# A mixture's routing with the last two batches one turn further apart, and second-choice rows added tile by tile

## The chip, the cores and the metric

The kernel runs on one core of a Trainium2 chip. The metric is device microseconds of one execution, as the median of several. A profile is a separate execution under the hardware profiler, with its own time. The engines are named as in the profile: PE (TensorE), DVE (VectorE), ACT (ScalarE), POOL (GpSimd) and SP (SyncE, which only issues transfers here).

## The reference

Activations of 4 batches by 512 tokens by 128 features go through four layers. Each is a half-weighted mixture of experts or gated block, an attention or scan, and the same mixture again. All is float32. What the change touches is the mixture of the last layer, which stands once before and once after that layer's attention:

```python
def _moe_forward(x, wg, w1, b1, w2, b2):          # T = 2048 tokens, E = 8, K = 2, H = 512
    cap = int(K * CAP_FACTOR * ((T + E - 1) // E))    # 512 slots for each expert
    scores = jax.nn.softmax(xt @ wg, axis=-1)
    gates_k, idx_k = jax.lax.top_k(scores, K)
    gates_k = gates_k / jnp.sum(gates_k, axis=-1, keepdims=True)
    m = jnp.transpose(jax.nn.one_hot(idx_k, E), (1, 0, 2)).reshape(K * T, E)
    loc = jnp.sum((jnp.cumsum(m, axis=0) - 1) * m, axis=-1).reshape(K, T).T
    valid = loc < cap                                 # first choices of all tokens, then second choices
    disp = zeros((E, cap, D)).at[idx_k, clip(loc)].add(xt * valid)
    h = jax.nn.relu(einsum('ecd,edh->ech', disp, w1) + b1)
    out = einsum('ech,ehd->ecd', h, w2) + b2
    return einsum('tk,tkd->td', gates_k * valid, out[idx_k, loc])
```

A token's place at its expert is its rank among all tokens that chose that expert, so the batches are ranked one after the other; second choices take the places behind the first ones.

## The kernel before

**Tiles.** A batch is four tiles of 128 tokens. The class `Mixture` makes one mixture in three steps: `tokens` (routing and scatter), `experts`, `combine`. There are four: f00 and f01 with one choice (layer 0), f30 and f31 with two (layer 3). f30 is the "third mixture", before the last attention; f31 is the last stage of the kernel.

**Routing.** `tokens` is a generator; each `yield` ends a turn. For one batch it does, in order: layer norm (statistics on DVE, L160 and L161; rs, rstd and off on POOL, L164 to L169; the norm itself on ACT, L174), four transposes on PE (L187) and a copy nT (L313), eight small matmuls for the logits (L322), the two choices on DVE (L218 to L231, with the exponential on ACT, L340), a running count (scan L354 and cum L388), the rank as six matmuls on PE (L365, L367, L371), and on DVE kept, at, slot and to (L392 to L401), the row of the scatter table for every token. Then POOL copies the gates beside the rows (L405) and issues the scatters to DRAM (L408), four for each choice and batch. The rank of a batch needs `cum`, the counts of the batches before it.

**Order.** In the stage before f30, `behind` runs the second layer's blocks for two pairs of batches. The first pair's tokens go through one generator with each scatter in a turn of its own. The second pair's batches 2 and 3 have one generator each, run by `skewed`: one turn of each live generator in every round, batch 3 starting some rounds after batch 2. In this stage POOL keeps the order in which the program issues its instructions; for PE, DVE, ACT and SP a planner sets the order when the kernel is built, in view of the order of issue. At run time every engine goes through its instructions in order, so one that waits holds all behind it. Copies of attention weights (wmixed, L901, and wqkvT, L134) are placed among the end of this stage.

**Experts.** When f30 or f31 is scattered, SP fetches for each expert two tables of 512 rows (L439), one for each choice, as four tiles of 128 rows by W = 130 columns. First choices are laid from the front of an expert's places and second ones from the end, so `behind[:, e, s]`, a flag of 0 or 1 for each row, says whether the second table's row counts. In a first-choice row the 128 features come first and two columns (place and gate) last; in a second-choice row the two columns come first. `prepare(e)` merges both on DVE:

```python
nc.vector.tensor_tensor(d2, d2, bc(behind[:, e, :], [P, per, W]), ALU.mult)      # L449
nc.vector.tensor_tensor(d[:, :, :D], d[:, :, :D], d2[:, :, 2:], ALU.add)         # L450
nc.vector.tensor_tensor(d[:, :, D:], d[:, :, D:], d2[:, :, :2], ALU.add)         # L451
```

Then PE transposes the four tiles (dT, L455), ACT copies dT to SBUF (L457), and DVE makes the rows for the way back (lost, L461; back, L464). The expert itself is the up product h_f (L479), a relu on ACT (L483) and DVE (L484), the down product o_f (L515), the bias on DVE (L495), the gate on ACT (L500) and the scatter of results on POOL (L501). `prepare(e + 1)` is issued after the h_f of expert e. Each of the two tables has three buffers; the next fetch into one waits for its last reader.

Of the kernel before, what the change touches and what calls it, by code (L numbers as in the profile page):

```python
# [12 lines left out]
ALU = mybir.AluOpType  # L13
# [4 lines left out]
P = 128  # L18
D = 128
# [11 lines left out]
W = D + 2  # L31
# [10 lines left out]
def kernel(ctx: ExitStack, tc: tile.TileContext, a: dict, out: bass.AP):  # L42
    nc = tc.nc
# [12 lines left out]
    def bank(name):  # L56
        return psum.tile([P, 512], FP, name=name, tag="bank", bufs=8)
# [147 lines left out]
    def bc(ap, shape):  # L205
        while len(ap.shape) < len(shape):
            ap = ap.unsqueeze(len(ap.shape))
        return ap.to_broadcast(shape)
# [28 lines left out]
    class Mixture:  # L237
# [180 lines left out]
        def experts(self, w, beside=None):  # L418

            w1, b1T, w2, b2 = w  # L420
            cap, per, whole, left = self.cap, self.per, self.cap // P, self.cap % P
            with tc.tile_pool(name=f"moe_{self.tag}", bufs=2) as pool:
                if self.k == 2:
# [5 lines left out]
                    behind = pool.tile([P, E, per], FP, name=f"behind_{self.tag}", tag="behind", bufs=1)  # L429
# [14 lines left out]
                def prepare(e):  # L444
                    tag = f"{e}_{self.tag}"
                    d = got[e, 0]
                    if self.k == 2:
                        d2 = got[e, 1]
                        nc.vector.tensor_tensor(d2, d2, bc(behind[:, e, :], [P, per, W]), ALU.mult)  # L449
                        nc.vector.tensor_tensor(d[:, :, :D], d[:, :, :D], d2[:, :, 2:], ALU.add)  # L450
                        nc.vector.tensor_tensor(d[:, :, D:], d[:, :, D:], d2[:, :, :2], ALU.add)  # L451
                    ps = bank(f"dT{tag}")
                    for s in range(per):
                        m = min(P, cap - s * P)
                        nc.tensor.transpose(ps[:, s * P : s * P + m], d[:m, s, :D], ident[:m, :m])  # L455
                    dT = pool.tile([P, cap], FP, name=f"dT{tag}", tag="dT")
                    nc.scalar.copy(dT, ps[:, :cap])  # L457

                    back = pool.tile([P, per], I32, name=f"back{tag}", tag="back", bufs=8)
                    lost = pool.tile([P, per], FP, name=f"lost{tag}", tag="lost", bufs=4)  # L460
                    nc.vector.scalar_tensor_tensor(  # L461
                        lost, d[:, :, D], 0.0, astray[:, e * per : (e + 1) * per], ALU.is_equal, ALU.mult
                    )
                    nc.vector.tensor_tensor(back, d[:, :, D], lost, ALU.add)  # L464
                    made[e] = d, dT, back
# [4 lines left out]
                for e in range(E):  # L470
# [3 lines left out]
                    d, dT, back = made[e]  # L474
# [12 lines left out]
                    if e + 1 < E:  # L487
                        prepare(e + 1)
# [83 lines left out]
    def padded(pool, i):  # L572
        v = pool.tile([P, NT, NH, SLOT], FP, name=f"vpad{i}", tag=f"vpad{i}", bufs=1)
        nc.gpsimd.memset(v, 0.0)
        nc.gpsimd.memset(v[:, :, :, HD : HD + 1].rearrange("p t h o -> p (t h o)"), 1.0)
        return v
# [435 lines left out]
    def prep_l1():  # L1012
        l1["gate"] = load_T(a["L1_ffn_gate_weight"], E, D, "gate1T")
        l1["wg"] = load_T(a["L1_ffn_w_gate"].rearrange("e i h -> (e i) h"), E * I1, D, "wg1T")
        l1["wu"] = load_T(a["L1_ffn_w_up"].rearrange("e i h -> (e i) h"), E * I1, D, "wu1T")
        l1["sg"] = load_T(a["L1_ffn_ws_gate"], D, D, "sg1T")
        l1["su"] = load_T(a["L1_ffn_ws_up"], D, D, "su1T")
        sd = load_T(a["L1_ffn_ws_down"], D, D, "sd1T")
        raw = stage.tile([P, E, I1], FP, name="raw_wd1", tag="raw")
        nc.sync.dma_start(raw, a["L1_ffn_w_down"].rearrange("e h i -> h e i"))  # L1020
        ps = bank("wd1")
        for c in range(NC):
            nc.tensor.transpose(
                ps[:, c * P : (c + 1) * P], raw[:, 2 * c : 2 * c + 2, :].rearrange("p e i -> p (e i)"), ident
            )
        wd = pools["w"].tile([P, NC, D], FP, name="wd1T", tag="wd1T")
        copy(wd, ps.rearrange("p (c d) -> p c d", d=D))
        l1["down"] = [wd[:, c, :] for c in range(NC)] + [sd]

        raw = stage.tile([P, D], FP, name="raw_qk1", tag="raw")  # L1030
        for i, s in enumerate(("q", "k")):
            nc.sync.dma_start(raw[i * NH * R1 : (i + 1) * NH * R1, :], a[f"L1_attn_W{s}1"])
        ps = bank("qk1")
        nc.tensor.transpose(ps[:, :D], raw, ident)
        qk1 = pools["w"].tile([P, D], FP, name="qk1T", tag="qk1T")
        copy(qk1, ps[:, :D])
        l1["factors"] = [qk1] + [load_T(a[f"L1_attn_W{s}2"], NH * R2, D, f"w{s}2T") for s in ("q", "k")]
        l1["wv"] = load_T(a["L1_attn_Wv"], D, D, "wv1T")
        l1["wo"] = load_T(a["L1_attn_Wo"], D, D, "wo1T")
        l1["bo"] = load_row(a["L1_attn_bo"], "bo1")  # L1040
# [339 lines left out]
    l3 = {}  # L1380
# [83 lines left out]
    def whole(parts):  # L1464
        for _ in parts:
            pass

    def skewed(gens, lag):

        live = {i: g for i, g in enumerate(gens)}  # L1470
        r = 0
        while live:
            for i in list(live):
                if r >= i * lag and next(live[i], "end") == "end":
                    del live[i]
            r += 1
            yield
# [24 lines left out]
    with tc.tile_pool(name="tables", bufs=1) as tables:  # L1502
# [19 lines left out]
        f30 = Mixture("f30", CAP3, 2)  # L1522
        l0_attn(f00.combine, emptied(f01, f30), lambda b: f01.tokens([b], gate0T, fine=True))
    with tc.tile_pool(name="weights12", bufs=1) as mid:
        pools["w"] = mid
        prep_l1()
        with tc.tile_pool(name="raw2", bufs=1) as pool:
            made = prep_l2(pool)
            next(made)
            next(made)  # L1530
            f01.experts(l0["w"], made.send)
            whole(made)
        first = small.tile([P, 1], FP, name="first_sigmoid", tag="first_sigmoid", bufs=1)
        nc.scalar.activation(first, l2["m"][:, 0, 0:1], AF.Sigmoid)
        for b in range(NB):
            whole(f01.combine(b))
        with tc.tile_pool(name="ahead1", bufs=2) as ahead:
            vpads[:] = [padded(ahead, 0), None]
            begun = l1_begin(ahead)

            def followed(pool, bs):
                yield from l1_ffn(pool, 0, bs)
                if bs[0] == 0:

                    yield from begun[0](0)
                    for g in range(2):
                        begun[1](0, g)
                        yield
                        begun[4][0, g] = begun[2](0, g)

            with tc.tile_pool(name="ffn10", bufs=2) as pool:
                whole(skewed([followed(pool, bs) for bs in pairs], 12))

            l1_attn(lambda pool: prep_l3_ffn(xs[0]), begun)

        def behind(pool, bs):
            yield from l1_ffn(pool, 1, bs)
            yield from l2_ffn(pool, 0, bs)
            yield from l2_attn(pool, bs)
            yield from l2_ffn(pool, 1, bs)  # L1560
            if bs[0] == 0:

                parts = f30.tokens(bs, l3["gate"], "scalar", pool, apart=True)
                while next(parts, "end") != "end" and next(parts, "end") != "end":
                    yield
            else:
                yield from skewed([f30.tokens([b], l3["gate"], "scalar", pool) for b in bs], 3)

        with tc.tile_pool(name="chain", bufs=2) as pool:
            decay = pool.tile([P, S], FP, name="decay", tag="decay", bufs=1)  # L1570
            nc.gpsimd.memset(decay, 0.9)
            for bs in pairs:
                l2["gates", bs[0]] = pool.tile([P, 2 * NT, P], FP, name=f"gates{bs[0]}", tag=f"gates{bs[0]}", bufs=1)
                nc.gpsimd.memset(l2["gates", bs[0]], 0.0)

            l2["row"] = []
            for u in range(E // 4):
                flag = pool.tile([P, 1], FP, name=f"flag{u}", tag=f"flag{u}", bufs=1)
                nc.vector.tensor_reduce(flag, ident.rearrange("p (r c) -> p r c", c=SLOT)[:, :, u], AX.X, ALU.add)
                row = pool.tile([P, P], FP, name=f"row{u}", tag=f"row{u}", bufs=1)  # L1580
                nc.vector.tensor_copy(row, flag.to_broadcast([P, P]))
                l2["row"].append(row)
            with tc.manual_schedule(engines={mybir.EngineType.Pool}):
                whole(skewed([behind(pool, bs) for bs in pairs], 8))
        pools["w"] = wpool
# [54 lines left out]
```

## Time and profile before

| | us |
|---|---|
| median of three runs (1532.04 to 1535.4) | 1533.77 |
| the profiled execution | 1513.06 |
| its span, first to last instruction | 1511.3 |
| granted TensorE clock in it, mean share of full speed | 0.911 |

| stretch of the span | us | PE busy | DVE busy | POOL busy | granted clock |
|---|---|---|---|---|---|
| batches 2 and 3 are routed, up to batch 2's first scatter (974.9 to 991.5) | 16.6 | 7.69 | 6.65 | 8.28 | 0.75, then 0.50 |
| their scatters (991.5 to 1013.4) | 21.9 | 3.51 | 3.97 | 16.46 | 0.50 |
| fetch and first preparation of f30 (1013.4 to 1021.25) | 7.85 | 1.09 | 3.42 | 4.69 | 0.50 |
| experts of f30 (1021.25 to 1075.3) | 54.05 | 54.05 | 25.91 | 25.36 | 0.97 |
| fetch and first preparation of f31 (1423.65 to 1430.06) | 6.41 | 1.09 | 3.33 | 0.00 | 0.50 |
| experts of f31 (1430.06 to 1484.5) | 54.44 | 54.44 | 24.87 | 25.24 | 0.96 |

Times in the span are microseconds from its start, durations of single instructions nanoseconds where so marked. A line of a timeline gives start, duration, engine, source line and operation, what is written and read, how often, and in brackets the idle time of that engine before it and what ended it. In the chain of waits each line is a start, a duration and the work that the next line waited for. Where a wait has several causes, the named one is the last by this profile and may not be the one that counted. L numbers are lines of the kernel before; in the changed kernel the edited operation stands at L450 to L454, and lines behind it are three higher.

### The profile page before, as it was taken

Reading aid. Unit: us, or ns where it says so; the run is one execution under the profiler, and the core shown is the slowest. Engines: PE = TensorE matmul, PEld = TensorE weight load, DVE = VectorE, ACT = ScalarE, POOL = GpSimd, SP = SyncE. Lnnn points to the kernel's source line nnn. Section 1 sums busy time; section 2 is a strip of 40 time slices with the busy share of each in tenths; the row PEclk is TensorE's granted clock in tenths of the full one; section 3 lists DMA queues with packets and bytes.
Section 4 is the critical chain, followed back from the end, with each engine's and each line's share of the span. In section 5 each row is a group of like instructions: output and inputs, shape, how many; then the busy total and the mean of one; then the engine's idle time right before and its main releaser. Section 6 shows DMA issues by size and latency. Waiting matters only on the chain.

```text
span 1511.3 us, 28774 instructions
## 1 busy us (share of the span) xinstructions
PE 1271.2 (84%) x10645; PEld 816.7 (54%) x10645; DVE 880.3 (58%) x2890; ACT 682.8 (45%) x1431; POOL 694.0 (46%) x808
## 2 busy tenths in 40 slices
PE   4787999995969999999878878729689999998394
PEld 3465666774746666667555656616433333333173
DVE  5236767763355657767456566525367787774343
ACT  1235877871422367767522222103236655564042
POOL 5346767871433678868323111464431223312343
PEclk9897999995999999999999888759879999999597
DMA  9410240002513884231022000023105000000223
GB/s 262 101 53 22 79 170 12 9 7 73 151 37 65 223 258 145 87 121 44 4 64 49 1 1 1 28 71 91 60 15 177 15 7 10 14 3 15 78 78 112
DMA packets 100660, 106.21 MB, mean 70 GB/s; under 512 B 9084, under 2 KB 73832, under 8 KB 100520
## 3 DMA queue, kind: packets, MB, share of 16 engines
q1 hardware_dynamic: 91752, 90.11, 20.7%
q0 software_dynamic: 6656, 13.22, 2.5%
q8 instruction: 84, 1.38, 0.4%
q10 hardware_dynamic: 2112, 1.05, 0.3%
q14 instruction: 56, 0.46, 0.1%
HBM read 62.49 MB, written 41.85 MB: 69 GB/s over the span
## 4 chain that ended last, share of the span: by engine, by line
PE 70%; DVE 9%; POOL 8%; DMA 5%; issue 5%; ACT 3%; SPq 1%; POOLq 0%; ACTq 0%; DVEq 0%
PE s_a L610 13%; PE t_a L655 10%; PE o_f L515 6%; PE h_f L479 6%; PE acc_a L677 5%; PE acc_a L749 5%; PE y_f L1329 3%; PE t_a L610 3%; POOL disp_f L408 2%; PE ot_a L768 2%; PE gu_f L1092 2%; PE lg_f L322 1%; POOL rstd_f L165 1%; DVE low L699 1%; PE gu_f L1093 1%
## 5 line engine op out<-in xcount | busy, mean ns | idle before, releaser
L642 POOL TENSOR_SCALAR sc_a<-sc_a,top_a 128x128 f32<-128x128 f32 (+3 forms) x256 | 274.8, 1089 | 84.7 <-DVE top_a L627 55.8
L610 PE MATMUL s_a<-k_a,q_a 32*128 32x512 f32 (+3 forms) x1536 | 263.4, 544 | 7.0 <-DVE top_a L631 3.7
L719 ACT ACTIVATE w_a<-t_a 128x512 f32<-128x512 f32 x256 | 140.4, 595 | 116.6 <-PE t_a L610 86.9
L699 DVE TENSOR_REDUCE low<-s_a 128x1 f32<-128x512 f32 x256 | 163.4, 684 | 45.4 <-PE t_a L610 32.7
L655 PE MATMUL t_a<-ident,sc_a 128*128 128x128 f32 x1280 | 174.3, 283 | 4.3 <-DVE top_a L631 3.8
L610 PE MATMUL t_a<-ql_a,k_a 32*128 32x512 f32 x512 | 167.2, 644 | 0.3 <-DVE low L699 0.2
L501 POOL DMA_INDIRECT res_f<-y_f,back_f x112 | 109.8, 980 | 124.6 <-ACT y_f L500 90.3
L655 PEld LDWEIGHTS t_a<-ident,sc_a 128*128 128x128 f32 x1280 | 144.6, 144 | 41.0 <-issue 16.5
L644 ACT ACTIVATE sc_a<-sc_a,top_a 128x128 f32<-128x128 f32 (+3 forms) x256 | 135.0, 575 | 12.8 <-DVE top_a L631 12.2
L610 PEld LDWEIGHTS s_a<-k_a,q_a 32*128 32x128 f32 x1536 | 91.5, 187 | 79.1 <-issue 41.9
L664 ACT ACTIVATE w_a<-t_a 128x256 f32<-128x256 f32 (+2 forms) x192 | 94.2, 526 | 71.0 <-PE t_a L655 70.8
L408 POOL DMA_INDIRECT disp_f<-n_f,to_f x96 | 94.8, 988 | 56.2 <-issue 35.8
L515 PE MATMUL o_f<-w_l,h_f 128*128 128x128 f32 (+1 forms) x896 | 109.6, 277 | 0.0
L515 PEld LDWEIGHTS o_f<-w_l,h_f 128*128 128x128 f32 (+1 forms) x896 | 102.1, 184 | 8.0 <-DVE back_f L464 4.4
L479 PE MATMUL h_f<-dT_f,w_l 128*128 128x320 f32 (+1 forms) x256 | 104.1, 544 | 2.8 <-ACT dT_f L457 2.8
L677 PE MATMUL acc_a<-w_a,vpad 128*32 128x128 f32 x2560 | 98.2, 280 | 0.0
L666 ACT COPY w_a<-t_a 128x256 f32<-128x256 f32 (+2 forms) x192 | 93.5, 527 | 5.0 <-PE t_a L655 4.7
L631 DVE CUSTOM_DVE_ANT_0 sc_a<-s_a,future 128x128 f32<-128x128 f32 (+3 forms) x128 | 62.3, 487 | 47.7 <-PE s_a L610 39.0
L1147 POOL TENSOR_TENSOR h_f<-h_f,cb_f 128x512 f32<-128x512 f32 x32 | 40.7, 1286 | 104.4 <-DVE h_f L1098 62.7
L631 DVE CUSTOM_DVE_ANT_0 sc_a<-s_a,table 128x128 f32<-128x128 f32 (+3 forms) x128 | 62.3, 487 | 43.5 <-PE s_a L610 38.3
L500 ACT ACTIVATE y_f<-o_f,d_f 128x128 f32<-128x128 f32 (+1 forms) x112 | 39.0, 394 | 98.0 <-DVE o_f L495 94.1
L749 PE MATMUL acc_a<-w_a,vpad 128*32 128x256 f32 x1024 | 82.1, 391 | 1.0 <-DVE low L699 0.9
(341 smaller groups left out, 2182.8 us busy)
## 6 DMA issues: line engine op xcount, KB each, us to landing
fac_a<-fac_a_sb SPq DMA_DIRECT2D x36, 256.0 KB, 4.9
disp_f<-zeros_f SPq DMA_DIRECT2D x4, 2080.0 KB, 10.6
d_f<-disp_f SPq DMA_DIRECT2D x32, 260.0 KB, 3.0
w_l<-in_L_ffn_w_dram SPq DMA_DIRECT2D x16, 512.0 KB, 7.2
cb_f<-rows_f SPq DMA_DIRECT2D x16, 512.0 KB, 8.4
q_a<-fac_a SPq DMA_DIRECT2D x32, 256.0 KB, 3.5
k_a<-fac_a SPq DMA_DIRECT2D x32, 256.0 KB, 3.8
r_f<-res_f SPq DMA_DIRECT2D x16, 256.0 KB, 2.8
```

The costliest lines, as they stand in the source:

```text
L408: nc.gpsimd.indirect_dma_start(out=self.to[c][i0 + t][:, :], out_offset=bass.IndirectOffsetOnAxis(ap=to[:, c, t : t + 1], axis=0), in_=ns[ ...
L479: nc.tensor.matmul(ps[u][:, :cap], w1[:, e, (c + u) * P : (c + u + 1) * P], dT, start=True, stop=True)
L515: nc.tensor.matmul(po[:m, s, :], h[:, c, s * P : s * P + m], w2[:, e, c, :], start=(c == 0), stop=(c == NC - 1),)
L610: nc.tensor.matmul(ps[:, n0:n1], q[r : r + SLOT, i * P : (i + 1) * P], k[r : r + SLOT, n0:n1], start=True, stop=True)
L631: nc.vector.tensor_tensor_reduce(sc, banks[r][:, :n], more, -1.0, HUGE, ALU.add, ALU.min, top)
L642: nc.gpsimd.tensor_scalar(sc, sc, top, None, ALU.subtract)
L644: nc.scalar.activation(sc, sc, AF.Exp, bias=top, scale=-1.0)
L655: nc.tensor.transpose(ps[:, x * n + j * P : x * n + (j + 1) * P], st["sc", u, i, r0 + x][:, j * P : (j + 1) * P], ident,)
L677: nc.tensor.matmul(st["acc", u][r * SLOT : (r + 1) * SLOT, i * P : (i + 1) * P], vpads[b % 2][:, j, g * 4 + r, :], st["w", u, i, r][:, j * ...
L699: nc.vector.tensor_reduce(st["low", u][:, i, c : c + 1], ps, AX.X, ALU.max, negate=True)
L719: nc.scalar.activation(w, ps, AF.Exp)
L749: nc.tensor.matmul(acc[r * SLOT : (r + 1) * SLOT, n0:n1], vpads[b % 2][:, j, g * 4 + r, :], st["w", u, j, r][:, n0:n1], start=(j == 0 and ...
```

## The change

Two edits. In `behind`, batch 3's routing begins four rounds after batch 2's instead of three. In `prepare`, the whole second-choice table is no longer multiplied by its flag and then added; for each of the four tiles one operation multiplies the 128 features of a second-choice row by the row's flag and adds them to the first-choice row. Only the two columns beside them are still multiplied and added for all four tiles at once. The edit in `prepare` holds for both f30 and f31.

```diff
@@ prepare(e), in experts
                     if self.k == 2:
                         d2 = got[e, 1]
-                        nc.vector.tensor_tensor(d2, d2, bc(behind[:, e, :], [P, per, W]), ALU.mult)
-                        nc.vector.tensor_tensor(d[:, :, :D], d[:, :, :D], d2[:, :, 2:], ALU.add)
+                        for s in range(per):
+                            nc.vector.scalar_tensor_tensor(
+                                d[:, s, :D], d2[:, s, 2:], behind[:, e, s : s + 1], d[:, s, :D], ALU.mult, ALU.add
+                            )
+                        nc.vector.tensor_tensor(d2[:, :, :2], d2[:, :, :2], bc(behind[:, e, :], [P, per, 2]), ALU.mult)
                         nc.vector.tensor_tensor(d[:, :, D:], d[:, :, D:], d2[:, :, :2], ALU.add)
                     ps = bank(f"dT{tag}")
@@ behind(pool, bs)
             else:
-                yield from skewed([f30.tokens([b], l3["gate"], "scalar", pool) for b in bs], 3)
+                yield from skewed([f30.tokens([b], l3["gate"], "scalar", pool) for b in bs], 4)
```

`skewed`, which the number goes to:

```python
def skewed(gens, lag):
    live = {i: g for i, g in enumerate(gens)}
    r = 0
    while live:
        for i in list(live):
            if r >= i * lag and next(live[i], "end") == "end":
                del live[i]
        r += 1
        yield
```

## Prediction

> **What bounds the kernel now.** I read the page first (PE 84% busy, 70% of the chain of waits), then the chain around the two third-layer mixtures, then each engine's timeline there. The scatter stage ahead of the third mixture (f30) is not PE's. In the chain of waits from 930 to 1100 us (start, duration, what):
>
> ```profile
> 982.85 0.23 POOL rs_f L164
> ...
> 984.83 0.50 ACT n_f L174
> 985.37 1.63 PE T_f L187 x4
> 987.00 0.32 PE rank_f L365 x2
> ...
> 990.54 0.10 DVE to_f L401
> ...
> 996.72 1.07 POOL disp_f L408
> ...
> 1011.14 2.27 DMA disp_f<-n_f,to_f
> ...
> 1015.39 4.41 DMA d_f<-disp_f
> ...
> 1021.25 5.35 PE h_f L479 x8
> ```
>
> Batch 3's norm and transposes stand ahead of batch 2's rank, then come the scatters, the fetch and the experts. The timelines of DVE and POOL say why:
>
> ```profile
> 981.96 0.19 DVE L388 TENSOR_TENSOR cum_f<-cum_f,pre_f 128x16 f32<-128x16 f32 x1
> 988.21 0.22 DVE L392 SCALAR_TENSOR_TENSOR kept_f<-rank_f,masks_f 128x64 f32<-128x64 f32 x1 [6.07 <-PE rank_f L371]
> 990.48 0.17 DVE L401 TENSOR_TENSOR to_f<-slot_f,spare_f 128x8 int32<-128x8 f32 x1
> 991.50 1.12 POOL L408 DMA_INDIRECT disp_f<-n_f,to_f  x1 [6.46 <-DVE masks_f L226]
> 1002.28 0.98 POOL L408 DMA_INDIRECT disp_f<-n_f,to_f  x1 [0.17 <-POOL wmixed_l L901]
> ```
>
> Batch 2's choices were finished at 982.15, but DVE then sat 6.07 us until its rank had left PE, where it was queued behind batch 3's transposes (985.37). POOL sat 6.46 us with nothing to scatter, and then issued batch 2's and batch 3's 16 scatters back to back, 1.26 us apart, to 1012.10. The end of this stage is set by when that train starts.
>
> The other edit is read at the fourth mixture (f31), DVE and PE timelines:
>
> ```profile
> 1426.69 0.70 DVE L449 TENSOR_TENSOR d_f<-d_f,behind_f 128x520 f32<-128x520 f32 x1 [16.10 <-DMA d_f<-disp_f]
> 1427.43 0.69 DVE L450 TENSOR_TENSOR d_f<-d_f,d_f 128x512 f32<-128x512 f32 x1
> 1428.22 1.09 PE L455 MATMUL dT_f<-ident,d_f 128*128 128x128 f32 x4 [18.63 <-DMA d_f<-disp_f]
> 1430.06 5.74 PE L479 MATMUL h_f<-dT_f,w_l 128*128 128x512 f32 x8 [0.75 <-ACT dT_f L457]
> ```
>
> PE does nothing until both whole-tile operations are through. By the order of instructions its wait is on L450 (end 1428.12); the DMA named is another that landed then. From 1430.06 PE is busy without a gap to 1484.5 (the stretch shows 54.44 of 54.44 us), as it is from 1021.25 to 1075.30 in f30: whatever starts the first expert earlier ends the stage earlier.
>
> [...] an idle TensorE falls back to half clock. The windows show it: granted clock 0.50 from 985.4 to 1021.25, so matmuls here are priced cold. [...] L408 lasts 0.96 us and lands 2.27 us after its start.
>
> **Part 1: four turns instead of three.** Nothing is added or removed. The order of instructions shows on PE batch 2's six rank matmuls ahead of batch 3's four transposes; on DVE batch 2's targets wholly ahead of batch 3's maxima, and two statistics of batch 3 moved between batch 2's choices; on POOL one of the two wmixed copies (L901, 0.30) ahead of batch 3's scatters instead of behind them. ACT and SP keep their order.
>
> Worked forward from the trace. The moved statistics put about 0.35 us into batch 2's choices: masks at 981.95, scan at 982.3. Batch 3's own statistics end at 980.0 instead of 979.16; POOL reads them at 982.85, behind six scatters, so that costs nothing. The rank starts at 982.0 and takes, cold, 0.69+0.43+0.43 (batch 3's at 992.75) = 1.55: 983.55. Targets: in f31 kept to L401 took 1.31 with 0.2 of other work between, so 1.1: 984.7. From targets to the first scatter took 0.81 (958.16 minus 957.35) and 0.85 (batch 2): **985.5, not 991.50**. POOL is free at 985.05.
>
> Batch 2's eight scatters then end at 985.5+10.08 = 995.6. Ahead of batch 3's stand two L405 (0.32), both wmixed (0.58) and a gap of 0.17: 996.67. Are batch 3's targets there? Its transposes stay at 985.37 (set by POOL's L169 and ACT), since the rank has left PE 1.8 us before; nT at 987.62, logits cold 1.88 as in f31 (1403.09): 989.5; maxima to masks 2.66 as in f31: 992.2; rank 1.55; kept to targets 1.9 with the wqkvT copy between: 995.7, plus 0.81 = 996.5. Just inside POOL's 996.67. So the last train starts at 996.7 instead of 1002.28: **-5.6 us**. After it stand only the last landing, the fetch and the experts, all released by it, and no other transfer runs there. Bounds: -4.6 if batch 3's targets are 1.2 us later than I work out; -6.0 if both trains keep their distance.
>
> **Part 2: rows times flag, tile by tile.** Per expert: out go L449 (128x520, 0.70) and L450 (128x512, 0.69); in come four scalar_tensor_tensor of 128x128 and one small multiply of 128x8 (0.16). L451 stays. 16 experts in both mixtures: 80 in for 32 out. No row has the new form. Pieces: a pointer operand adds 0.06 (L1368 749 against L1338 690 ns); at 128 columns, L178 with two of them lasts 0.34:
>
> ```profile
> 350.68 1.12 DVE L178 TENSOR_SCALAR n_f<-x,mv_f,rstd_f 128x128 f32<-128x128 f32 x4 [1.47 <-POOL rstd_f L165]
> ```
>
> I take these: first done at 0.34, fourth at 1.12, against 1.43 for the dependent pair. On top, each transpose now has its own wait for its own operation. In f31: first transpose at 0.40, four cold ones 1.09: through at 1.49 us after the data, against 2.62 before (1429.31 minus 1426.69). **-1.1**. In f30 the transposes came 0.32 after L450's end, where PE's first wait after the pools are exchanged is a long list: 0.66+1.09 = 1.75 against 2.83 (1020.45 minus 1017.62): **-1.1**. For the other seven experts nothing is won: PE is busy and their preparation lies under matmuls, 26 us of DVE work in 54. Bounds for each mixture: -0.35 if the transposes only run after the fourth operation (2.27 against 2.62); -1.3 with cheaper operations. [...] Behind the new DVE instructions stand the next expert's and the relu L484, which waits for PE anyway; behind the transposes' new waits stands, on PE, h_f of the first expert alone, since later experts' rows are ready before PE gets there. SP's fetches wait for the same last readers as before (L451, and ACT's L500), so the three buffers come free no later.
>
> **Sum:** -5.6 -1.1 -1.1 = -7.8 us. The profiled execution took 1513.06 (span 1511.3); it would take 1505.3. The runs' median is 1533.77, 1.4% more; the same steps at that pace are still about 7.8, so **1526.0**. About 0.2%, 3 us, is what can be told from no change.
>
> **Rivals.** (A) Only one part works. Part 1 alone gives 1528.2. That is the case if the pointer operands or the small waits on PE eat the tile-by-tile gain. Part 2 alone gives 1531.6, if batch 3's targets come so late that POOL's second train does not start earlier. For it: my two paths to 996.7 differ by 0.2. Against it: POOL would have to lose 5.6 there, while to 995.6 it has batch 2's train, which nothing of batch 3 holds. (B) Slower: TensorE's clock. Its granted mean is 0.911. If less idle ahead of the experts brought a lower grant over the two blocks of 54 us, a fall by 7% there (0.97 to 0.90) costs 7.8 us and cancels the gain; beyond 10% it is slower by over 3: about 1537. Against it: from 1200 to 1300 PE is 99.9% busy at a granted 1.00, so load does not lower it here. (C) The planner does not do what the call says. It does: the order on PE shows the swap; and outside the two stretches the order on all five engines is the same, so no other stage is at risk. What is left of it is a time of about 1533, if something that no view here shows holds the last landing.
>
> **How the numbers follow.** Forecast 0.78; (A) 0.13, of which part 2 alone, 0.05, lies at the edge of telling; (B) 0.04; (C) 0.05. Faster 0.90, same 0.06, slower 0.04. Range: the bounds give -5.3 (4.6+0.35+0.35) to -8.6 (6.0+1.3+1.3); with the runs' own spread of 1.7: 1523.5 to 1530.2. I go down to 1522.5, since the timed runs hold 20 us that the profiled one does not, and waits of this stage may be longer there; and up to 1531.0 to take in most of part 1 alone with that spread.
>
> **What would show it.** Right: the first L408 of batch 2 near 985.5; the wait of 6.07 us for the rank gone from DVE and batch 3's norm no longer ahead of it in the chain; the first h_f of f30 at 1014.5 instead of 1021.25 (-6.7), of f31 at 1422.2 (-7.8), which is 2.3 us after its first DVE operation instead of 3.37. Wrong: POOL idle again between the two trains (batch 3 late); the four operations over 0.4 us apart, or transposes bunched behind the last; a granted clock below 0.94 in the two blocks of experts.

## The result and the profile after

On one chip, in 12 runs of each kernel, the median went from 1531.82 to 1526.43 us: a ratio of 0.9956 (95% interval 0.9938 to 0.9975), which is 3.8 to 9.5 us. In a second set of runs, on another chip, it was 0.9932 (0.9907 to 0.9957). The ratio is estimated together with its interval and isn't the quotient of the two medians, which is 0.9965 in the first set and 0.9944 in the second. The prediction was 1526.0, faster, with a sum of -7.8 us.

Times of different chips can't be put beside each other here: beside the 1531.8 us of the first set, the kernel before has medians of 1535.9 and 1534.8 us on two chips and of 1513.8 and 1515.0 on two others. The two profiled executions (1513.06 and 1516.23) even stand the other way round. So ratios are taken on one chip, and profiles are compared by stretches between the same instructions. *a* is the first of the six scatters (L408) of batches 0 and 1 that follow batch 2's norm on POOL. Lengths in us, worked out from starts and ends in the timelines; the last two columns are second profiles of the two kernels, on another chip:

| stretch | before | after | before again | both again |
|---|---|---|---|---|
| start to *a* (no edit) | 974.89 | 974.67 | 979.54 | 982.13 |
| *a* to first h_f of f30 | 46.36 | 39.79 | 46.65 | 40.61 |
| first to last h_f of f30 | 57.48 | 58.95 | 59.04 | 58.60 |
| on to the first rows of f31 (no edit) | 347.96 | 356.04 | 361.93 | 359.00 |
| rows to first h_f of f31 | 3.37 | 2.42 | 3.36 | 2.42 |
| first to last h_f of f31 | 57.87 | 58.06 | 58.04 | 58.03 |
| on to the end | 23.42 | 24.59 | 24.73 | 24.77 |

The edited stretches are 6.57 and 0.95 us shorter in the first pair, 6.04 and 0.94 in the second. The stretches without an edit differ by up to 14 us between executions, which is what hides a gain of 7 in a single pair.

The chain of waits after, from 974 to 1022 us (start, duration, what):

```profile
982.94 1.04 POOL rstd_f L165
...
996.40 0.63 POOL disp_f L408
...
1005.25 2.28 DMA disp_f<-n_f,to_f
...
1009.51 4.27 DMA d_f<-disp_f
...
1014.46 6.40 PE h_f L482 x8
```

PE's transposes and rank are gone from it; from *a* to the last scatter it is POOL alone, with its issue times. DVE's timeline after:

```profile
982.78 0.22 DVE L392 SCALAR_TENSOR_TENSOR kept_f<-rank_f,masks_f 128x64 f32<-128x64 f32 x1 [1.06 <-issue]
...
983.78 0.17 DVE L401 TENSOR_TENSOR to_f<-slot_f,spare_f 128x8 int32<-128x8 f32 x1
...
995.39 0.17 DVE L401 TENSOR_TENSOR to_f<-slot_f,spare_f 128x8 int32<-128x8 f32 x1
```

The wait for batch 2's rank is 1.06 instead of 6.07 us: PE starts on it at 981.23, where before it came to it only at 986.79, behind the transposes, though the counts were there at 982.15. POOL's timeline, the first scatter of each train:

```profile
985.16 1.12 POOL L408 DMA_INDIRECT disp_f<-n_f,to_f  x1 [0.33 <-POOL n_f L405]
...
996.40 0.98 POOL L408 DMA_INDIRECT disp_f<-n_f,to_f  x1 [0.47 <-issue]
```

POOL idles 0.33 us ahead of batch 2's train instead of 6.46. And f31, DVE, then PE:

```profile
1429.45 1.14 DVE L450 SCALAR_TENSOR_TENSOR d_f<-d_f,behind_f,d_f 128x128 f32<-128x128 f32 x4 [16.28 <-DMA d_f<-disp_f]
```

```profile
1429.90 1.22 PE L458 MATMUL dT_f<-ident,d_f 128*128 128x128 f32 x4 [17.74 <-DMA d_f<-disp_f]
1431.87 5.91 PE L482 MATMUL h_f<-dT_f,w_l 128*128 128x512 f32 x8 [0.75 <-ACT dT_f L460]
```

The first transpose starts 0.45 us after the first operation instead of 1.53, and the four (1.22 us) run between the operations.

### The profile page after: what moved, and what is told of

Read it like the earlier page. It is cut to its first block, busy times and chain, and to the rows that moved or that the text cites. A ratio compares the mean times of both kernels' runs of the same rounds, so it can differ in the third digit from the quotient of the medians.

```text
span 1514.5 us, 28821 instructions
## 1 busy us (share of the span) xinstructions
PE 1272.7 (84%) x10645; PEld 816.2 (54%) x10645; DVE 878.5 (58%) x2938; ACT 682.5 (45%) x1431; POOL 691.4 (46%) x808
## 3 DMA queue, kind: packets, MB, share of 16 engines
q10 hardware_dynamic: 2112, 1.05, 0.3%
## 4 chain that ended last, share of the span: by engine, by line
PE 64%; POOL 9%; DVE 9%; DMA 7%; issue 7%; ACT 3%; SPq 1%; another core or an unknown queue 0%; POOLq 0%; ACTq 0%; DVEq 0%
PE s_a L613 13%; PE t_a L658 9%; PE h_f L482 5%; PE acc_a L680 5%; PE o_f L518 5%; PE acc_a L752 5%; PE y_f L1332 3%; PE t_a L613 3%; POOL disp_f L408 2%; DMA cb_f<-rows_f 2%; PE ot_a L771 2%; POOL res_f L504 2%; POOL rstd_f L165 1%; DVE low L702 1%; PE qk_a L924 1%
## 5 line engine op out<-in xcount | busy, mean ns | idle before, releaser
L504 POOL DMA_INDIRECT res_f<-y_f,back_f x112 | 106.7, 952 | 129.4 <-ACT y_f L503 93.8
L408 POOL DMA_INDIRECT disp_f<-n_f,to_f x96 | 94.8, 987 | 50.4 <-issue 36.7
```

The lines of the kernel that those rows point to most:

```text
L408: nc.gpsimd.indirect_dma_start(out=self.to[c][i0 + t][:, :], out_offset=bass.IndirectOffsetOnAxis(ap=to[:, c, t : t + 1], axis=0), in_=ns[ ...
L504: nc.gpsimd.indirect_dma_start(out=self.back[e * per + s][:, :], out_offset=bass.IndirectOffsetOnAxis(ap=back[:m, s : s + 1], axis=0), in_ ...
```

## The experiments

**The kernel before once more, and both edits once more** (one chip, no edit to either).

> The kernel before once more, unchanged: a null for the measurement and a second profiled execution. The first one (1513.06 us) lies 20 us under the median of its timed runs, and every other profile so far shows jumps against it in stretches that no edit touches: +4.2 to +4.3 us between 941 and 975, +2.4 to +5.0 between 1309 and 1329, +2.6 to +4.9 between 1370 and 1391. If that first execution was a lucky one, this profile shows the same jumps and a span near 1530; if the edits cause them, it has none of them and a span near 1513. As a null: ratio 1.000 within 0.002; a ratio of 0.996 would mean that the tile edit's measured gain of 6 us is not the edit's.

Measured: 1534.7 against 1534.81, ratio 1.000 (0.9982 to 1.0018). The profiled run took 1535.04. The edited stretches are close to those of the first profile of before (46.65 and 3.36 for 46.36 and 3.37), and the jumps in untouched stretches are there too: the page of before was taken in an execution without them, and they come without the edits. Why they come on some chips wasn't settled.

> Both edits once more, unchanged, beside the others on one chip. The two edits alone gave ratios of 0.9943 (lag) and 0.9961 (tiles), both together 0.9956 on another chip. If the parts add up as I predicted (5.6 and 2.2 us), the ratio is 0.995; if the single runs are to be taken at their word (8.8 and 6.0), it is 0.990; if either edit alone brings what both bring, 0.995 to 0.996 with the profile still showing 39.8 us from the first scatter behind batch 2's norm to f30's first h_f.

Measured: 1526.24, ratio 0.9932 (0.9907 to 0.9957), between the first two of the three forecasts. *a* to h_f is 40.61: batch 2's first scatter comes 11.37 us after *a* instead of 10.49, since here its targets (ready at 992.65) and not POOL were last. The starts of the two trains lie 0.7 to 0.9 us later here; the gain is 6.04 instead of 6.57.

**Each edit alone**, twice, on two chips.

```diff
 lag alone:    -  yield from skewed([... for b in bs], 3)
               +  yield from skewed([... for b in bs], 4)
 tiles alone:  the new prepare(e), with skewed(..., 3)
```

> Four turns alone, the whole-tile pair L449/L450 kept. Measure in the profile: from the first of the six scatters (L408) that follow batch 2's norm on POOL to f30's first h_f: 46.36 us before (974.89 to 1021.25), 39.79 with both edits (974.67 to 1014.46). My theory (batch 2's rank ahead of batch 3's transposes is all of part 1): 46.36 - 5.5 = about 40.9 here, the data-to-h_f stretches unchanged at 3.6 (f30) and 3.37 (f31); time about 5.6 us under the kernel before, ratio 0.9963. Rival (the two edits need each other, or only the tile edit works): 46.4 and a ratio of 1.000.

> The tile-by-tile operation alone, three turns kept. My theory: first h_f of f30 comes 2.55 instead of 3.63 us after the first operation on its rows, that of f31 2.42 instead of 3.37 us; the scatter trains as before, so from the first scatter behind batch 2's norm to f30's first h_f 46.4 - 1.1 = 45.3 us; time 2.0 to 2.2 us under the kernel before, ratio 0.9986, which lies at the edge of what can be told. Rival (the operations take time from DVE inside the expert blocks, which comes back as a loss): gaps on PE in the expert blocks and a ratio of 1.000 or above.

> The lag edit alone once more. Its runs gave 0.9943 (0.9923 to 0.9963), 8.8 us, where its profile shows 5.1 us less from the first scatter behind batch 2's norm to f30's first h_f (41.51 against 46.65). Scatter between executions: nearer to 0.9966. A gain in another place: 0.994 again.

> The tile edit alone once more. Its runs gave 0.9961 (0.9947 to 0.9974), 6 us, where its two starts in the profile (1.07 and 0.95 us earlier) make 2.0. If the rest was scatter between executions (stretches that neither edit touches differ by up to 12 us between profiles), this comes nearer to 0.9987; if the edit also gains in some place that I don't see, 0.996 again, and this profile's stretch from the first qk after f30 to the rows of f31 is again short (333.4 us, against 340.2, 339.3 and 337.3 in the kernel before, with the lag alone and with both).

| | ratio, first chip | ratio, second chip | *a* to h_f f30 | rows to h_f f30 / f31 |
|---|---|---|---|---|
| lag alone | 0.9943 (0.9923 to 0.9963) | 0.9968 (0.9956 to 0.9981) | 41.51, 40.96 | 3.63 / 3.37 |
| tiles alone | 0.9961 (0.9947 to 0.9974) | 0.9992 (0.9976 to 1.0009) | 45.46, 45.72 | 2.55 / 2.42 |

In the profile the parts are clean and add up: against the profile of before on its kind of chip the lag takes 5.1 (46.65 to 41.51) and 5.4 us (46.36 to 40.96) from the first stretch and leaves the second alone; the tile edit takes 1.07 and 0.95 from rows to h_f. In time, the first chip gave both more than that (8.8 and 6.0 us), the second 4.9 and 1.2, close to what was forecast for the repeats (0.9968 for 0.9966, 0.9992 for 0.9987). With tiles alone the stretch from f30 to the rows of f31 was short on the first chip (355.06). On the second it is 348.22, the lag alone has 349.05 there, and the first profile of before 347.96: no gain. An interval from one chip holds its scatter there, not the difference between chips. In time the tile edit by itself is told from no change on the first chip and not on the second.

What the surplus of the first chip is stays open, since the repeat ran on a chip without the jumps. On the two chips that have them, this untouched stretch takes 361.04 to 361.93 us in the three profiles without the tile edit or with its order reversed (below), and 355.06 to 359.00 in the five with the tiles in order. A gain of 2 to 3 us there isn't ruled out; no run here shows a cause for it.

**Batch 3's norm behind batch 2's scatters**: eight turns. PE and ACT keep the order of four turns; on POOL L164 to L169 of batch 3 move behind batch 2's train.

> Both edits with eight turns instead of four. PE and ACT keep the order that four turns give; on POOL batch 3's norm (L164 to L169) now stands behind batch 2's eight scatters instead of ahead of them. If batch 3's norm on POOL is what the second train hangs on: batch 2's first scatter comes about 0.4 us earlier, its train ends near 995, and batch 3's norm, transposes, choices and targets follow it, so its first scatter comes 12 to 13 us later than with four turns (near 1009 on that clock); from the first scatter behind batch 2's norm to f30's first h_f 52 to 53 us instead of 39.8, time 12 us above both edits. If only the order on PE counts, 39.8 and no change.

Measured: 1540.43, ratio 1.0038 (1.0022 to 1.0054), 14.2 us above both edits on the same chip; *a* to h_f 53.94, 13.3 more. POOL's timeline:

```profile
993.98 0.98 POOL L408 DMA_INDIRECT disp_f<-n_f,to_f  x1 [3.41 <-DVE to_f L401]
...
1004.62 1.04 POOL L165 TENSOR_TENSOR rstd_f<-rs_f,mhalf 128x4 f32<-128x4 f32 x1
...
1018.05 1.12 POOL L408 DMA_INDIRECT disp_f<-n_f,to_f  x1 [0.92 <-DVE ends_f L262]
```

Batch 2's train starts 11.35 us after *a*, as with both edits (I had expected 0.4 earlier; the targets, not POOL, held it: it sat 3.41 us, time enough for the norm, which takes 1.95 with both edits). Then POOL computes batch 3's norm (from L164 at 1004.32) and stands idle until its choices are through: the whole path from norm to scatter, 13.7 us, lies bare between the trains. More turns are thus not better by themselves; five to seven were not run. Four put batch 2's rank ahead of batch 3's transposes on PE and still leave batch 3's norm ahead of batch 2's train on POOL, and it needs both.

**Where the tile edit's gain lies**: the operations of an expert in reversed order, and the single operation taken apart again, both with four turns.

```diff
 reversed:  -  for s in range(per):
            +  for s in reversed(range(per)):
 unfused:   -  scalar_tensor_tensor(d[:, s, :D], d2[:, s, 2:], behind[:, e, s : s + 1], d[:, s, :D], mult, add)
            +  tensor_tensor(d2[:, s, 2:], d2[:, s, 2:], bc(behind[:, e, s : s + 1], [P, D]), mult)
            +  tensor_tensor(d[:, s, :D], d[:, s, :D], d2[:, s, 2:], add)
```

> Both edits, but the four operations of an expert go from the last tile to the first, while the four transposes go from the first to the last: the first transpose then waits for the last operation. If the gain of the tile edit lies in the overlap of operations and transposes, the first h_f comes about 0.7 us later than with both edits: 3.1 us (f31) and 3.2 (f30) after the first operation. If it lies only in one operation having replaced two, nothing changes: 2.42 and 2.55.

> Both edits, but each tile's rows are multiplied and added in two operations (128x128 each, eight for an expert) instead of one. Eight at about 0.21 us apart: the fourth tile is there at about 1.8 us instead of 1.14. If cutting into tiles alone brought the gain, the first h_f of f31 comes 2.4 us after the first operation; if both the cut and the single operation are needed, about 3.0; the kernel before took 3.37.

Measured (one timed execution and profile of each, 1528.90 and 1528.97 us, too few to tell such steps by the time), rows to the first h_f of f31: 3.08 reversed and 3.00 unfused, against 2.42 with the edit and 3.37 before. PE reversed, then DVE and PE unfused:

```profile
1442.34 1.09 PE L458 MATMUL dT_f<-ident,d_f 128*128 128x128 f32 x4 [18.53 <-DVE d_f L453]
```

```profile
1440.73 0.49 DVE L450 TENSOR_TENSOR d_f<-d_f,behind_f 128x128 f32<-128x128 f32 x2 [16.15 <-DMA d_f<-disp_f]
...
1441.95 0.49 DVE L451 TENSOR_TENSOR d_f<-d_f,d_f 128x128 f32<-128x128 f32 x2
```

```profile
1441.53 1.45 PE L457 MATMUL dT_f<-ident,d_f 128*128 128x128 f32 x4 [17.95 <-DVE d_f L451]
```

Reversed, the operations start at 1441.11, and the four transposes follow in a block (1.09 us) 1.23 us later: of the 0.95, some 0.66 is overlap and 0.29 the cheaper operations. Unfused, PE starts early but the fourth tile comes 1.71 us after the first operation began (1442.44), and the transposes stretch to 1.45. The cut alone brings 0.37; it takes the single operation to bring the rest.

**Rival (B), and the first expert's clock.** PE was kept busy ahead of the experts of f30 and f31 (in these two mixtures only) with matmuls whose output nobody reads; 30, then 15, then 17 and 18:

```diff
+                    idle = bank(f"idle_{self.tag}")
+                    for _ in range(30):                  # 15; 17 in f30 and 18 in f31
+                        nc.tensor.matmul(idle, ident, w1[:, 0, :], start=True, stop=True)
                     n1 = pool.tile([P, E], FP, name=f"n1_{self.tag}", tag="n1", bufs=1)
```

> Both edits, and 30 matmuls of 128x512 whose output nothing reads, on PE between n_f (L426) and the first expert's transposes, where PE idles for 17 us in each of the last two mixtures (995.7 to 1012.6, 1412.2 to 1429.9); they are there in the first two only if the width fits (it is 320 there for the rows, the same matmul). If the clock is what the first expert loses, its eight h_f matmuls take 3.6 us instead of 6.40 and 5.91, the transposes a little less: 5 us for both mixtures, ratio about 0.992. If the clock pays for the extra work elsewhere (the rival of the prediction in which a busier PE is granted less), the granted clock in the expert blocks falls below 1.00 and the ratio is 0.995 or more. If the 30 take longer than the gap, the first transposes start later than 0.45 us after the first operation on the rows.

Measured: 1541.16, ratio 1.0034 (1.0020 to 1.0048). PE's timeline (lines stand 3 higher from here on):

```profile
1004.52 28.02 PE L429 MATMUL idle_f<-w_l,ident 128*128 128x512 f32 x60
...
1033.78 3.70 PE L485 MATMUL h_f<-dT_f,w_l 128*128 128x512 f32 x8 [0.80 <-ACT dT_f L463]
```

Each of these float32 matmuls is two instructions on PE (60 for 30), so they took 28 us where the gap is 17, and pushed the experts back by some 9.4 in each mixture. But h_f took 3.70 us instead of 5.98, and the grant didn't fall: it is 1.00 from 1025 to 1060. The busier PE lost no clock there, so (B) is refuted for these blocks.

> Both edits and 15 idle matmuls instead of 30 ahead of the experts of the last two mixtures. With 30 the profile showed 60 PE instructions for them, 28.0 us, some 11 us past the arrival of the first rows, after which the eight h_f took 3.70 us. Half of them is 30 x 0.43 = 12.9 us and 2 to 4 us for the start at half clock, 15 to 17 us in a gap of 17.4 and 17.7. If the clock stays up over the 1 to 2 us that are left: h_f in 3.7 us in both mixtures (5.98 and 5.89 without), the transposes through 0.3 us earlier, 5 us together, 1521 where both edits alone take 1526, ratio to the kernel before about 0.990. If the extra work is paid back elsewhere through a lower grant: a clock below 1.00 in the expert blocks, and 1526 or more. If the clock falls back in the 1 to 2 us: h_f at 6 us and no change.

Measured: 1507.32, ratio 0.9955 (0.9939 to 0.9971). The 30 instructions took 15.59 us, h_f still 5.36 and 5.81. The windows say why (length, busy time of PE, weight loads, DVE, ACT, POOL, granted clock, DMA share, GB/s):

```profile
1013.00:1016.10 3.10, 0.93 (x5) 0.48 (x4) 1.71 (x8) 0.58 (x1) 1.52 (x5) 1.00 1.09 287
1016.10:1019.50 3.40, 3.34 (x4) 1.51 (x5) 3.04 (x15) 0.69 (x2) 0.00 (x0) 0.50 0.69 170
```

PE had been idle for 2.17 of 3.1 us, and the next 3.4 us were granted half: the third of the forecasts. (This run and the next were on chips on which the kernel with both edits and nothing more was not run, so only ratios to the kernel before, and stretches, can be put beside it.)

> Both edits and idle matmuls that fill the gap to its end: 17 in f30, 18 in f31. With 15 they ended 1.4 us (f30) and 2.9 us (f31) ahead of the first transposes and the eight h_f still took 5.36 and 5.81 us; with 30 they ran straight into the transposes and h_f took 3.70. At 0.86 us each and 2 to 2.7 us for the start at half clock, 17 and 18 end within 0.5 us of the first rows. If an unbroken PE is what keeps the clock, h_f takes 3.7 us in both mixtures: 1.7 to 2.3 us less than with both edits in each, less up to 0.5 us of overrun, so 3 to 4 us together and a ratio to the kernel before near 0.993. If the 0.8 us wait for the copy of the transposed rows is enough to lose it, h_f stays at 5.4 to 6 us and the ratio at 0.995.

Measured: 1509.39, ratio 0.9964 (0.9945 to 0.9983), no better than both edits. The first half of the forecast came true and the second did not. PE, then DVE:

```profile
1013.89 3.70 PE L485 MATMUL h_f<-dT_f,w_l 128*128 128x512 f32 x8 [0.80 <-ACT dT_f L463]
...
1021.21 5.04 PE L521 MATMUL o_f<-w_l,h_f 128*128 128x128 f32 x30 [2.96 <-DVE h_f L490]
```

```profile
1020.33 0.17 DVE L456 TENSOR_TENSOR d_f<-d_f,behind_f 128x8 f32<-128x8 f32 x1 [2.04 <-DMA d_f<-disp_f]
1020.41 1.40 DVE L490 TENSOR_SCALAR h_f<-h_f,b1T_l 128x512 f32<-128x512 f32 x2
```

h_f takes 3.70 us in both mixtures. Then PE waits 2.96 us for the relu on DVE (L490 there, L487 with both edits), because ahead of the relu DVE's queue holds the small multiply of a later expert's rows, which waits 2.04 us for their landing (h_f was through at 1017.59, the relu began at 1020.41). With both edits it is DVE that waits there, 1.79 us for h_f: the half clock had covered the landing. With DVE's order as it is, the arrival of the rows is now the bound, and the idle costs the clock once more (2.55 us idle from 1017.4 to 1020.8, then 0.50 to 1024.2). From rows to the last h_f of f30 it took 62.86 us (2.38 and 60.48) where both edits take 61.50 and 61.15; in f31, with a wait of 1.69 for the relu, 60.28 and 60.48 and 60.45. A DVE order with the relu ahead of that multiply was not run. No run clearly beat both edits.

## Why the prediction was right

By its own steps, in the first profile after:

- **Batch 2's train.** Predicted 985.5, measured 985.16. Against *a* that is 10.6 and 10.49. That it is so near is partly luck, for I had the targets last (984.7, and 0.81 to the scatter). Here they were ready at 983.95, and POOL was last: its L405 ended at 984.84, and the scatter followed 0.33 later. With both edits again the targets were last (11.37), so which path holds this train differs between executions.
- **Batch 3's train.** Predicted 996.7, measured 996.40. I had POOL last (996.67) and the targets 0.2 ahead of it. Here the targets were last (995.56, and 0.84 to the scatter), while on the second chip both edits had POOL last (wmixed ends at 1004.39, scatter at 1004.55). That the two paths are nearly of one length was the right reading: to shorten the longer one alone would bring 0.3 us here and 0.5 there (an estimate: POOL's path gives 996.10 for 996.40 with the gap of 0.17, the targets' path 1004.01 for 1004.55 with 0.85).
- **Part 2.** Predicted fourth operation at 1.12 us, measured 1.14; first transpose of f31 at 0.40, measured 0.45; h_f 2.3 after the rows, measured 2.42. The last term was short by 0.12: each transpose waits for its own operation, so the four take 1.22 and not the 1.09 of a block. In f30 1.75 to the last transpose, as predicted. The price of smaller operations can be read from the profile of before: a `tensor_tensor` took 693 ns at 128x512 (L450) and 292 at 128x128 (L397), so four quarters at that price are 1.17 us for 0.69 (an estimate from these two); a `scalar_tensor_tensor` of 128x512 on two tiles in SBUF took 686 ns (L1369), no more than L450. The four of the edit, 128x128 with a pointer operand, take 1.14 us together.
- **The sum.** First h_f of f30 -6.57 against *a* (predicted -6.7), f31 -0.95 (predicted -1.1): -7.5 for -7.8. By the runs with one edit, the lag brought 5.1 and 5.4 of the 5.6. The first ratio gives -6.7 us, the second -10.4, both with -7.8 inside the interval. That the median of 1526.43 lies so near 1526.0 is luck in part: the kernel before had 1531.82 in that set, and I had counted from 1533.77.
- **Rival (A)**, only one part works: refuted in the profile for both parts; in time the tile part alone is told from none on one of two chips, and the prediction had put it at the edge of telling. **(B)**: refuted. **(C)**: refuted; the trains moved by what was said.

What the sum didn't hold is the first expert's h_f. In the first pair it takes 6.40 instead of 5.35 us, which gives back 1.05 of the 6.57. The windows after:

```profile
1012.50:1016.20 3.70, 2.83 (x6) 1.52 (x7) 3.08 (x17) 0.58 (x1) 0.03 (x1) 0.50 0.99 260
1016.20:1019.90 3.70, 3.70 (x6) 1.51 (x5) 2.26 (x11) 0.69 (x1) 0.00 (x0) 0.50 0.55 144
1019.90:1023.30 3.40, 3.40 (x27) 2.88 (x26) 0.82 (x2) 1.27 (x2) 0.00 (x0) 1.00 0.03 5
```

Full clock comes 7.4 us after the first transpose, in the profile of before 5.2. It doesn't take the edits: the kernel before again has 6.44 us for that h_f, tiles alone 5.21 and 5.65, both edits again 5.98. It varies by up to 1.2 us between executions for this start (5.21 to 6.44); no run was made to find what sets it, and a range for a single execution should hold it.

## What to carry to other kernels

When two batches share queues, find for each engine which of the two its queue serves first, and aim for the order in which the later batch's slow preparation runs under the earlier batch's transfers; a step too far (here eight turns) lays it bare and costs more than was won. Cutting an operation in tiles paid where the reader works tile by tile and stands idle; for the experts whose preparation lies under a busy PE it showed no gain (57.48 to 59.04 us from first to last h_f of f30 without the edit, 57.79 to 58.95 with it). Price an edit of half a per cent by stretches between fixed instructions, and on more than one chip, since untouched stretches differed here by more than the gain.

## What the runs showed of the hardware that I had not expected

The way from the first transpose to full clock took between 4.96 and 7.44 us in 22 starts from idle (f30 and f31, in the 11 profiles without idle matmuls). That is a spread of 2.5 us. With 15 and with 17 matmuls half clock came in f30 for a stretch of 3.4 us, with 1.00 on both sides (1016.1 to 1019.5 and 1020.8 to 1024.2). Idle time of 0.8 us within 4.9 did not lose the clock once it was up (with 17 matmuls, 1012.50 to 1017.40, granted 1.00 there and in the next 3.4 us), nor did the 1.69 us ahead of the relu in f31 of that run (1.00 from 1423 to 1480); 2.2 us within 3.1 did (with 15, 0.50 in the next 3.4 us). And keeping PE at full clock brought no gain, since the half clock had been covering a late transfer: h_f was 2.3 us shorter than with both edits again (3.70 for 5.98), and PE then waited 2.96.
